# Three ternary weight buffers and a hand-given VectorE order in the gated stage of a hybrid block

## The chip, the cores and the metric

One core of a Trainium2 chip runs the kernel. The metric is the device time of one execution in microseconds, lower is better. Engines are named as in the profile: PE (TensorE matmuls), PEld (its weight loads), DVE (VectorE), ACT (ScalarE), POOL (GpSimd) and SP (SyncE, which here issues the DMAs). 128x512 means 128 partitions by 512 elements.

## The reference

A block of four residual steps on x of 2 x 1024 rows by D = 512; each step takes the layernorm of x.

```python
x = x + attn_a(layernorm(x), w_in, w_out)     # gated stage
x = x + ffn(layernorm(x), w_gate_up, w_proj)  # feed-forward 0
x = x + attn_b(layernorm(x), ...)             # softmax attention
x = x + ffn(layernorm(x), w_gate_up, w_proj)  # feed-forward 1

# attn_a: 16 heads of 32, chunks of 64 rows
q, k, v, a, g = split(x @ w_in.T, 5)
q = q * rsqrt(mean(q*q) + eps);  k = tanh(k)
a = clip(sigmoid(a + 2), 0.6, 0.9995);  u = k * v
prefix = cumprod(a)                            # inside a chunk
mem = prefix * (state + cumsum(u / max(prefix, 1e-6)))
y = sigmoid(g) * (q * mem) + (1 - sigmoid(g)) * v
return y @ w_out.T

# ffn: the weights are made ternary in groups of 64
scale = mean(abs(w));  w = clip(round(w / scale), -1, 1) * scale
h = silu(x @ w_gate.T) * (x @ w_up.T)
return rms_norm(h) @ w_proj.T
```

## The kernel before, in words

The change lies in the first stage (the gated attention, L182 to L430) and in its border with feed-forward 0.

The 2048 rows are four units t of 512 rows. x stays in SBUF as 16 tiles of 128 rows (xres). For a unit, `Input` measures the rows (layernorm statistics on DVE, a square root on ACT), scales them (`normal`, xn_a on DVE), and PE transposes them (`turn`, xnt_a) for ACT to copy (a_xt). `queries` (L273) then projects q in four column tiles c, squares it on ACT, and sums the squares per head on PE (pss); a root on ACT and three DVE steps (L300 to L304) make the factor rq. The loop over t and c (L335 to L407) projects k and v (kv), a and g (ag), each 8 matmul calls for a half of 512 columns; PE's order is the program's. Behind the projections stands a chain for each c: ACT makes u, v, a and gate; DVE clips a, scans it (prefix), POOL multiplies u by prefix, DVE scans again (mem), multiplies by qn (L391, from pr, a product on PE that spreads rq over the heads) and by gate, and POOL subtracts and adds v, which gives yt. In the very last chain the POOL steps are on DVE (`other`, L366). After the four c come the output products a_out (L421), in which yt is multiplied by w_out, and DVE adds them to x (L426). The queries of the next unit are put ahead of these output products.

In the gaps of this stage the feed-forward weights are made ternary. `Ternary` (L144) holds one chunk f of 16: three tiles of 128x512 loaded to the tile w (L155), their absolute values mag (L157) and signs (L159) on ACT; `mean` (L162) is a small product pm on PE and a copy to scale on ACT; `finish` (L169) is six DVE steps over 128x1536 (L171 to L179). `quantise(0..2)` does the means, `quantise(3)` finishes the chunk, stores it to DRAM (L319) and begins the next, whose load waits for a buffer. w, mag, sign and scale have two buffers each. At L345 `pieces` says which of these calls stands behind which projection.

Feed-forward 0 begins with 16 loads of those chunks into SBUF (L569) and with the layernorm and transposition of its first four tiles (xn_f, xnt_f, xs, L570 to L573); the statistics of these tiles are taken in the last unit (L398). Each chunk is then 8 matmuls g, 8 u and 8 f_out.

What sets the order: PE follows the program in the gated stage (`manual_schedule`, L323) until `order.close()` (L415). DVE follows it only for the first input (L326); elsewhere the scheduler places DVE, ACT, POOL and SP instructions by its own estimates when the kernel is built, and each engine then works its queue in the order built. PSUM for single products and transpositions is a pool of four banks (`bank`), for kv and ag two tiles (`big`).

Of the kernel before, what the change touches and what calls it, by code (L numbers as in the profile page):

```python
# [17 lines left out]
P = 128  # L18
D = 512
# [23 lines left out]
def kernel(  # L43
# [31 lines left out]
    def bank(name):  # L75
        return ps_pools[-1][1].tile([P, BLK], F32, tag="bank", name=name)
# [4 lines left out]
    def load_x(lo, hi):  # L81
        for i in range(lo, hi):
            nc.sync.dma_start(out=xres[i], in_=x[ts(i, P), :])
# [55 lines left out]


# [3 lines left out]
    class Ternary:  # L144
# [3 lines left out]
        def __init__(self, pool, f, tiles):  # L148
            self.pool, self.f, self.n = pool, f, f"{f}_{tiles[0]}"
            self.shape = [P, len(tiles), D]  # L150
            self.w = pool.tile(self.shape, F32R, tag="w32", name=f"w32_{self.n}")
            w32 = self.w.bitcast(F32)
            for i, e in enumerate(tiles):
                src = w_pt[ts(f, P), :] if e == 2 else w_gu[e * NF + f].rearrange("p c n -> p (c n)")
                nc.sync.dma_start(out=w32[:, i, :], in_=src)  # L155
            self.mag = pool.tile(self.shape, BF, tag="mag", name=f"mag{self.n}")
            nc.scalar.activation(self.mag, w32, AF.Abs)  # L157
            self.sign = pool.tile(self.shape, BF, tag="sign", name=f"sign{self.n}")
            nc.scalar.sign(self.sign, w32)  # L159
            self.scale = None  # L160

# [20 lines left out]
    with ExitStack() as s:  # L182
# [8 lines left out]
        def load_w_in(i):  # L191
            w = w_in.tile([P, NKC, D], F32, tag=f"w_in{i}", name=f"w_in{i}")
            nc.sync.dma_start(
                out=w, in_=w_in_t[:, ts(i, D)].rearrange("(c p) n -> p c n", p=P)
            )
            return w

        w_q, w_k, w_v = (load_w_in(i) for i in range(3))
# [6 lines left out]
        chunk = [Ternary(tp, 0, range(3))]  # L205
        w_a, w_g = (load_w_in(i) for i in (3, 4))
        load_x(TPB, 2 * TPB)
        w_out = wa.tile([P, NKC, D], F32, name="w_out")
        nc.sync.dma_start(out=w_out, in_=w_out_t.rearrange("(c p) n -> p c n", p=P))

# [62 lines left out]
        def queries(t, xt):  # L273

            q = ap_.tile([P, NKC, BLK], F32, tag="q", name=f"q{t}")
            pss = bank(f"pss{t}")
            late = []

            def mean_square(c, sq):
                nc.tensor.matmul(  # L280
                    pss, headmean[:, c, :], sq, start=(c == 0), stop=(c == NKC - 1)
                )

            for c in range(NKC):
                pq = bank(f"pq{t}_{c}")
                project(pq, w_q, c, xt)
                nc.scalar.copy(q[:, c, :], pq)
                sq = ap_.tile([P, BLK], F32, tag="sq", name=f"sq{t}_{c}")
                nc.scalar.square(sq, pq)
                if late:  # L290
                    mean_square(*late.pop())
                late.append((c, sq))
                if c < 3 and t:
                    quantise(c)
                elif c and not t:
                    quantise(c - 1)
            mean_square(*late.pop())
            rq = ap_.tile([16, BLK], F32, tag="rq", name=f"rq{t}")
            nc.scalar.activation(rq, pss[:16, :], AF.Sqrt, bias=rms_eps[:16])
            nc.vector.reciprocal(rq, rq)  # L300
            parts = rq_parts[t % 2]
            hi, lo = parts[:16], parts[32:48]
            nc.vector.tensor_copy(hi, rq)
            nc.vector.tensor_sub(lo, rq, hi.bitcast(F32))  # L304
            quantise(3)
            return q, parts

        load_x(2 * TPB, NTT)

        def quantise(i):  # L310

            now = chunk[0]
            if now is None:
                return
            if i < 3:
                now.mean(i, bank)
                return
            now.finish(now.w)
            nc.sync.dma_start(out=w_kept[now.f].bitcast(F32), in_=now.w.bitcast(F32))  # L319
            chunk[0] = Ternary(tp, now.f + 1, range(3)) if now.f + 1 < NF else None  # L320

        order = ExitStack()
        order.enter_context(tc.manual_schedule(engines={mybir.EngineType.PE}))  # L323
        before = [None] * NKC
        first = Input(0, at_once=False)
        with tc.manual_schedule(engines={mybir.EngineType.DVE}):  # L326
            for j in range(TPB + 1):
                if j < TPB:
                    first.measure(j)
                if j:  # L330
                    first.normal(j - 1)
                    first.turn(j - 1)
        xt = first.xt
        q, rq = queries(0, xt)
        for t in range(NBLK):  # L335
            yt = wa.tile([P, NKC, BLK], F32, tag="yt", name=f"yt{t}")
            following = None
            for c in range(NKC):
                n = f"{t}_{c}"
                kv, ag = big(f"kv{n}"), big(f"ag{n}")  # L340
                project(kv[:, 0, :], w_k, c, xt)
                project(kv[:, 1, :], w_v, c, xt)

                if t < NBLK - 1:
                    pieces = ((2,), (), (3,)) if c % 2 else ((0,), (1,), ())  # L345
                else:
                    pieces = ((0, 1), (2,), (3,)) if c < NKC - 1 else ((), (), ())
                for i in pieces[0]:
                    quantise(i)
                project(ag[:, 0, :], w_a, c, xt)  # L350
                project(ag[:, 1, :], w_g, c, xt)
                for i in pieces[1]:
                    quantise(i)
                if following and c > 1:
                    for j in (2 * c - 4, 2 * c - 3):
                        following.turn(j)
# [9 lines left out]
                other = nc.gpsimd if (t, c) < (NBLK - 1, NKC - 1) else nc.vector  # L366
# [12 lines left out]


# [6 lines left out]

                pr = bank(f"pr{n}")
                nc.tensor.matmul(pr, headrow[:, c, :], rq, start=True, stop=True)
                qn = ap_.tile([P, BLK], F32, tag="qn", name=f"qn{n}")  # L390
                nc.vector.tensor_mul(qn, pr, q[:, c, :])  # L391
# [4 lines left out]

                if t + 1 == NBLK and c == 0:
                    ff_stats = layernorm_stats(range(TPB), "f0_0")  # L398
                if t + 1 < NBLK and c < 2:
                    if c == 0:  # L400
                        following = Input(t + 1)
                    following.normal(0 if c == 0 else 1)
                for i in pieces[2]:
                    quantise(i)
                if following and c == 2:
                    following.normal(2)
                    following.normal(3)  # L407

            if following:
                xt = following.xt  # L410
                q_next, rq_next = queries(t + 1, xt)
            products = [(j, k) for j in range(TPB) for k in range(NKC)]
            if not following:

                order.close()  # L415
                products.sort(key=lambda jk: jk[1] == NKC - 1)
            po = {}
            for j, k in products:
                if k == 0:
                    po[j] = bank(f"a_out{t}_{j}")  # L420
                nc.tensor.matmul(  # L421
                    po[j], yt[:, k, ts(j, P)], w_out[:, k, :], start=(k == 0), stop=(k == NKC - 1)
                )
                if k == NKC - 1:
                    xi = xres[t * TPB + j]
                    nc.vector.tensor_add(xi, xi, po[j])  # L426
                    if following:
                        quantise(j)
            if following:
                q, rq = q_next, rq_next  # L430

    edge_sb = ctx.enter_context(tc.tile_pool(name="edge", bufs=1, reuse_waits="tile"))
# [20 lines left out]
    class FeedForwardInput:  # L455


        def __init__(self, which, t, pool, tag, stats=None):
            self.n = f"{which}_{t}"
            self.which, self.tiles = which, range(t * TPB, (t + 1) * TPB)  # L460
            self.stats = stats or layernorm_stats(self.tiles, f"f{self.n}")
            self.xs = pool.tile([P, 2, NKC, BLK], F32R, tag=tag, name=f"xs{self.n}", bufs=1)
            self.xn = {}

        def normal(self, j):
            i = self.tiles[j]
            self.xn[j] = normal(i, j, self.stats, f"f{self.which}_{i}")

        def tile(self, j, psum):
            if j not in self.xn:  # L470
                self.normal(j)
            pt = transposed(self.xn.pop(j), f"f{self.which}_{self.tiles[j]}", psum)
            hi, lo = (self.xs[:, e, :, ts(j, P)] for e in range(2))
            nc.scalar.copy(hi, pt)  # L474
            nc.vector.tensor_sub(lo, pt, hi.bitcast(F32))

# [5 lines left out]
    def feed_forward(which, store, first=None, beside=None):  # L482


        with ExitStack() as s:
# [84 lines left out]
            if not first:  # L570
                first = FeedForwardInput(which, 0, edge_sb, "xt", ff_stats)
                for j in range(TPB):
                    first.tile(j, ring)  # L573
# [44 lines left out]
        0, False, None,  # L618
# [533 lines left out]
```

## Time and profile before

| what | value |
|---|---|
| median of 3 runs | 2147.88 us (2146.33 to 2148.32) |
| profiled execution | 2146.65 us |
| its span, first to last instruction | 2144.9 us |
| mean granted PE clock | 0.996 |
| PE's idle time from 0 to 420 us | 23.5 us |
| gated stage: first q product to last output product | 12.38 to 393.44 us |
| first product of feed-forward 0 | 398.59 us |

The page says for every engine how long it was busy in the span; a view of waits says which engine waited for which instruction of which other one; a timeline lists instructions with their start and duration, and in brackets the idle time before them with what ended it. "x16" counts instructions: a matmul call on 32-bit data is two instructions. In a windows row the columns are: stretch, its length, PE, PEld, DVE, ACT and POOL busy (with counts), granted PE clock, share of DMA, GB/s. Idle time of an engine costs nothing unless PE or the end waits for it.

### The profile page before, as it was taken

Reading aid. Unit: us, or ns where it says so; the run is one execution under the profiler, and the core shown is the slowest. Engines: PE = TensorE matmul, PEld = TensorE weight load, DVE = VectorE, ACT = ScalarE, POOL = GpSimd, SP = SyncE. Lnnn points to the kernel's source line nnn. Section 1 sums busy time; section 2 is a strip of 40 time slices with the busy share of each in tenths; the row PEclk is TensorE's granted clock in tenths of the full one; section 3 lists DMA queues with packets and bytes.
Section 4 is the critical chain, followed back from the end, with each engine's and each line's share of the span. In section 5 each row is a group of like instructions: output and inputs, shape, how many; then the busy total and the mean of one; then the engine's idle time right before and its main releaser. Section 6 shows DMA issues by size and latency. Waiting matters only on the chain.

```text
span 2144.9 us, 28054 instructions
## 1 busy us (share of the span) xinstructions
PE 2108.8 (98%) x10615; PEld 1242.2 (58%) x10624; DVE 1069.1 (50%) x2272; ACT 835.2 (39%) x1590; POOL 449.8 (21%) x812
## 2 busy tenths in 40 slices
PE   8999999999999999999999999999999999999998
PEld 3444444688888854444444444444545447888887
DVE  5766686533343234555555465464546662433322
ACT  4444333234344322444444422243434523333333
POOL 1312212122122221111111113021212221121212
PEclk9999999999999999999999999999999999999999
DMA  6111211600000111111110101201110033000000
GB/s 255 59 59 62 86 59 74 250 1 1 1 1 1 35 46 37 41 26 41 23 44 21 46 8 37 57 20 42 24 32 15 14 111 132 20 1 20 1 20 20
DMA packets 50999, 98.71 MB, mean 46 GB/s; under 512 B 10800, under 2 KB 19120, under 8 KB 50864
## 3 DMA queue, kind: packets, MB, share of 16 engines
q1 hardware_dynamic: 50864, 96.93, 13.8%
q8 instruction: 83, 1.36, 0.3%
q14 instruction: 52, 0.43, 0.1%
HBM read 58.75 MB, written 16.78 MB: 35 GB/s over the span
## 4 chain that ended last, share of the span: by engine, by line
PE 83%; DVE 8%; DMA 4%; ACT 2%; issue 1%; POOL 1%; SPq 1%; DVEq 0%; ACTq 0%; POOLq 0%
PE y L904 12%; PE g L524 11%; PE u L524 11%; PE f_out L545 11%; PE s L805 10%; PE pq L737 8%; PE t L866 8%; PE pv L702 3%; PE b_out L965 2%; DMA w<-in_w_pt_dram 1%; DMA w_kept<-w 1%; DVE one L174 1%; PE kv L269 1%; DVE w L179 1%; PE ag L269 1%
## 5 line engine op out<-in xcount | busy, mean ns | idle before, releaser
L882 ACT ACTIVATE pr<-t 128x512 f32<-128x512 f32 (+3 forms) x768 | 314.8, 497 | 380.6 <-PE t L874 380.4
L815 DVE CUSTOM_DVE_ANT_0 s<-s,causal 128x128 f32<-128x128 f32 (+3 forms) x512 | 245.3, 510 | 126.1 <-PE s L805 117.4
L904 PE MATMUL y<-pr,val 128*64 128x512 f32 (+3 forms) x1536 | 291.6, 501 | 0.2 <-POOL pr L885 0.2
L539 POOL TENSOR_TENSOR ssq<-ssq,sq 128x512 f32<-128x512 f32 x120 | 155.9, 1299 | 603.6 <-ACT sq L538 603.6
L530 DVE TENSOR_TENSOR h<-h,u 128x512 f32<-128x512 f32 x128 | 88.0, 688 | 362.0 <-PE u L524 355.9
L524 PE MATMUL g<-xs,w 128*128 128x512 f32 x1024 | 262.4, 398 | 0.9 <-ACT xs L474 0.7
L545 PE MATMUL f_out<-w,hs 128*128 128x512 f32 x1024 | 257.7, 394 | 0.3 <-DVE hs L533 0.3
L820 DVE TENSOR_REDUCE nmax<-s 128x1 f32<-128x512 f32 x256 | 165.0, 686 | 184.4 <-PE s L805 184.3
L524 PE MATMUL u<-xs,w 128*128 128x512 f32 x1024 | 256.4, 392 | 0.0
L805 PE MATMUL s<-gr,gr 32*128 32x512 f32 (+3 forms) x1536 | 248.8, 492 | 2.6 <-DVE nmax L815 2.6
L524 PEld LDWEIGHTS u<-xs,w 128*128 128x128 f32 x1024 | 192.4, 188 | 43.5
L545 PEld LDWEIGHTS f_out<-w,hs 128*128 128x128 f32 x1024 | 191.6, 188 | 43.9 <-DVE hs L533 1.1
L524 PEld LDWEIGHTS g<-xs,w 128*128 128x128 f32 x1024 | 190.9, 189 | 44.0 <-ACT xs L474 0.9
L866 PE MATMUL t<-gr,gr 32*128 32x512 f32 (+3 forms) x1536 | 198.8, 533 | 0.0
L904 PEld LDWEIGHTS y<-pr,val 128*64 128x64 f32 x1536 | 93.5, 136 | 179.9 <-issue 105.7
L737 PE MATMUL pq<-b_xt,w_qk 128*128 128x512 f32 x384 | 176.0, 603 | 0.0
L805 PEld LDWEIGHTS s<-gr,gr 32*128 32x128 f32 x1536 | 147.6, 185 | 46.8 <-issue 14.0
L532 ACT CAST hs<-h 128x512 fp32r<-128x512 f32 x128 | 79.4, 621 | 236.6 <-DVE h L530 236.6
L885 POOL TENSOR_SCALAR_AFFINE_SELECT pr<-pr 128x256 f32<-128x256 f32 x256 | 101.3, 408 | 332.2 <-ACT pr L882 332.2
L529 ACT ACTIVATE h<-g 128x512 f32<-128x512 f32 x128 | 76.5, 598 | 224.3 <-PE g L524 224.1
L533 DVE TENSOR_TENSOR hs<-h,hs 128x512 fp32r<-128x512 f32 x128 | 88.6, 692 | 83.1 <-ACT hs L532 83.1
L737 PEld LDWEIGHTS pq<-b_xt,w_qk 128*128 128x128 f32 x384 | 69.6, 189 | 88.0 <-issue 74.0
(155 smaller groups left out, 2211.0 us busy)
## 6 DMA issues: line engine op xcount, KB each, us to landing
w<-w_kept SPq DMA_DIRECT2D x32, 768.0 KB, 8.7
w_kept<-w SPq DMA_DIRECT2D x16, 768.0 KB, 3.2
gr<-gr SPq DMA_DIRECT2D x96, 128.0 KB, 2.3
w<-in_w_gu_dram SPq DMA_DIRECT2D x32, 256.0 KB, 2.8
share<-ys SPq DMA_DIRECT2D x128, 64.0 KB, 2.0
w_in<-in_w_in_t_dram SPq DMA_DIRECT2D x5, 1024.0 KB, 11.2
x<-in_x_dram SPq DMA_DIRECT2D x16, 256.0 KB, 7.1
w<-in_w_pt_dram SPq DMA_DIRECT2D x16, 256.0 KB, 3.5
```

The source lines that it names most:

```text
L524: nc.tensor.matmul(po, ws[f][:, part, ts(k, P)], xs[:, e, k, :], start=(k == 0 and e == 0), stop=(k == NKC - 1 and e == 1),)
L533: nc.vector.tensor_sub(hp[:, 1, :], h, hp[:, 0, :].bitcast(F32))
L539: nc.gpsimd.tensor_add(ssq, ssq, sq)
L545: nc.tensor.matmul(po[j], hp[:, e, ts(j, P)], ws[f][:, 2, :], start=(f == 0 and e == 0), stop=(f == NF - 1 and e == 1),)
L737: nc.tensor.matmul(po, w[:, k, ts(kind, P)], xts[b][:, k, ts(e, BLK)], start=(k == 0), stop=(k == NKC - 1),)
L805: nc.tensor.matmul(part, queries[:, ts(j, P)], keys[:, first : first + nk], start=True, stop=True,)
L815: nc.vector.tensor_tensor_reduce(part, part, causal[:, BLK - part.shape[-1] :], -1.0, 3.0e38, ALU.add, ALU.min, top,)
L820: nc.vector.tensor_reduce(top, part, AX.X, ALU.max, negate=True)
L866: nc.tensor.matmul(banks[u, e][:, :nq], keys[:, ts(kb, P)], queries[:, (qb + 1) * BLK - nq : (qb + 1) * BLK], start=True, stop=False,)
L882: nc.scalar.activation(pr[:, e, :nq], banks[u, e][:, :nq], AF.Exp)
L885: nc.gpsimd.affine_select(out=pr[:, :, :P], in_=pr[:, :, :P], compare_op=ALU.is_ge, fill=0.0, base=0, pattern=[[0, 2], [1, P]], channel_mu ...
L904: nc.tensor.matmul(y[64 * e : 64 * e + 64, lo:], all_values[:, HV * (NH * kb + h) : HV * (NH * kb + h) + 64], pr[:, e, : BLK - lo], start= ...
```

## The change

Five edits, all in the gated stage and at its end.

1. The ternary weight tile w gets three buffers. Loading (`__init__`) and the work on it (`begin`) are parted; chunks 1 and 2 are loaded at the start, and finishing chunk f issues the load of f+3. w_q and w_k move to the pool `edge`, into the space that the feed-forward's first input takes later.
2. DVE's order is the program's in the whole stage (`fixed`). qn is written over q and is placed before the second scan; the next unit's input is measured at the end of the unit before.
3. The last sum of squares, the root (`roots`) and the factor (`factors`) go behind the first and second output product; transpositions of the next input stand between kv and ag.
4. Feed-forward 0's first input is made in the last unit: it is measured behind c=1 (two tiles normalised there), its tiles are transposed in c=3, two before ag and two between its halves.
5. Chunk 15 is finished behind the last additions to x; the last output products take k in the order (0, 1), 2, 3.

```diff
-            self.w = pool.tile(self.shape, F32R, tag="w32", name=f"w32_{self.n}")
+            self.w = pool.tile(self.shape, F32R, tag="w32", name=f"w32_{self.n}", bufs=3)
...
+        def begin(self):
...
+        w_qk = edge_sb.tile([P, 2, NKC, D], F32, tag="xt", name="w_in_qk")
...
-        chunk = [Ternary(tp, 0, range(3))]
+        chunk = [Ternary(tp, 0, range(3)).begin()]
         w_a, w_g = (load_w_in(i) for i in (3, 4))
         load_x(TPB, 2 * TPB)
+        chunk.append(Ternary(tp, 1, range(3)))
...
+        chunk.append(Ternary(tp, 2, range(3)))
...
+            rq = ap_.tile([16, BLK], F32, tag="rq", name=f"rq{t}", bufs=1)
+            def roots():
+                mean_square(*late.pop())
+                nc.scalar.activation(rq, pss[:16, :], AF.Sqrt, bias=rms_eps[:16])
+            def factors():
+                nc.vector.reciprocal(rq, rq)
...
-            chunk[0] = Ternary(tp, now.f + 1, range(3)) if now.f + 1 < NF else None
+            chunk.pop(0)
+            if chunk:
+                chunk[0].begin()
+            if now.f + 3 < NF:
+                chunk.append(Ternary(tp, now.f + 3, range(3)))
...
-        order.enter_context(tc.manual_schedule(engines={mybir.EngineType.PE}))
+        fixed = {mybir.EngineType.PE, mybir.EngineType.DVE}
+        order.enter_context(tc.manual_schedule(engines=fixed))
...
-                    pieces = ((0, 1), (2,), (3,)) if c < NKC - 1 else ((), (), ())
+                    pieces = (((0, 1), (2,), (3,)), ((0, 1), (2,), ()), ((), (), ()))[max(c - 1, 0)]
...
+                if not last and c > 1:
+                    for j in (2 * c - 4, 2 * c - 3):
+                        following.turn(j)
+                        if c == 2:
+                            following.normal(j + 2)
                 for i in pieces[0]:
                     quantise(i)
+                ff_tiles = range(TPB) if last and c == NKC - 1 else ()
+                turn = lambda name: bank(name)
+                for j in ff_tiles[:2]:
+                    ff_first.tile(j, turn, j + 2)
                 project(ag[:, 0, :], w_a, c, xt)
+                for j in ff_tiles[2:]:
+                    ff_first.tile(j, turn)
                 project(ag[:, 1, :], w_g, c, xt)
...
+                if last and c == NKC - 3:
+                    ff_first = FeedForwardInput(0, 0, edge_sb, "xt")
+                    ff_first.normal(0)
+                    ff_first.normal(1)
...
-                order.close()
-                products.sort(key=lambda jk: jk[1] == NKC - 1)
+                products.sort(key=lambda jk: max(jk[1], 1))
...
+                    if not last:
+                        if j == 0:
+                            roots()
+                        elif j == 1:
+                            factors()
                         quantise(j)
+            if last:
+                quantise(3)
+            if not last:
                 q, rq = q_next, rq_next
+                following = Input(t + 2) if t + 2 < NBLK else None
+        order.close()
```

The class `FeedForwardInput` moves ahead of the stage and takes a tile to normalise between the two steps of another:

```diff
+        def tile(self, j, psum, following=None):
...
             nc.scalar.copy(hi, pt)
+            if following:
+                self.normal(following)
             nc.vector.tensor_sub(lo, pt, hi.bitcast(F32))
```

## The prediction

> **What bounds the kernel now.** First the page: which engine is full. Then PE's waits in the stage that the change touches (0 to 420 us), since only they can be won.
>
> ```profile
> PE 2108.8 (98%) x10615; PEld 1242.2 (58%) x10624; DVE 1069.1 (50%) x2272; ACT 835.2 (39%) x1590; POOL 449.8 (21%) x812
> ```
>
> PE is busy 98% of the span: 36 us are idle in all, 23.5 of them before 420 us, and 6.8 of these before the first transposition. The other stages are not touched. PE's waits, in total us, times, longest:
>
> ```profile
> PE pm L166 <- ACT mag L157: 4.7, 2, 2.7
> PE pss L280 <- ACT sq L289: 3.4, 5, 2.1
> PE pq L269 <- ACT a_xt L265: 2.6, 4, 0.7
> PE xnt_f L136 <- DVE xn_f L127: 2.3, 2, 1.9
> PE a_out L421 <- POOL yt L395: 1.0, 1, 1.0
> ```
>
> pm on mag is the late ternary load (40 us and 352 us). The next view is the timeline at the second of these and at the end of the stage, with PE's clock in two windows of 2 us (the third number from the end):
>
> ```profile
> 355.06 1.01 PE L166 MATMUL pm<-mag,groupmean 128*128 128x512 bf16 x2 [2.68 <-ACT mag L157]
> ...
> 355.87 8.17 PE L269 MATMUL ag<-a_xt,w_in 128*128 128x512 f32 x16
> ```
>
> ```profile
> 356.00:358.00 2.00, 2.00 (x4) 0.88 (x3) 1.01 (x1) 2.00 (x5) 0.95 (x1) 0.50 0.04 8
> ```
>
> ```profile
> 376.73 0.33 SPq L319 DMA_DIRECT2D w_kept<-w  x1
> 377.17 19.11 SPq L569 DMA_DIRECT2D w<-w_kept  x16
> ...
> 393.49 0.69 DVE L426 TENSOR_TENSOR x<-x,a_out 128x512 f32<-128x512 f32 x1 [0.17 <-PE a_out L421]
> ...
> 397.29 0.63 PE L136 MATMUL xnt_f<-ident,xn_f 128*128 128x128 f32 x4 [1.95 <-DVE xn_f L127]
> ...
> 402.48 2.06 PE L524 MATMUL u<-xs,w 128*128 128x512 f32 x8
> ```
>
> After 2.68 us of idleness PE runs 3.4 us at half clock: the 16 ag matmuls take 8.17 us, 7.03 elsewhere. And feed-forward's 16 weight loads leave SP at 377.17, behind the last ternary store and 16 us ahead of the end of the output products (393.44), so they are hidden. Last, DVE's price for finishing a chunk, with POOL beside it and without:
>
> ```profile
> 58.85 2.70 DVE L174 SCALAR_TENSOR_TENSOR one<-scale,mag 128x1536 bf16<-128x1536 bf16 x1
> ...
> 59.90 2.78 POOL L367 TENSOR_TENSOR u<-u,v 128x512 f32<-128x512 f32 x1
> ...
> 125.71 1.76 DVE L174 SCALAR_TENSOR_TENSOR one<-scale,mag 128x1536 bf16<-128x1536 bf16 x1
> ```
>
> **What is removed.** Three weight buffers, issued one or two chunks ahead, remove the waits on mag (2.06 and 2.68) and the half clock behind the second (8.17-7.03, and 0.4 in the two pm: 1.55). pss of the last square goes behind the first output product, transpositions go ahead of ag: gone are five pss waits (3.4, one of them 2.07 because mag sat ahead of sq on ACT), three pq on a_xt (1.9), one pq on scale (0.68). yt for k=2 is no longer needed first (1.01). Sum 13.3 us. w_qk in another pool, rq with one buffer and qn written over q move no work; their waits are on long finished readers, cost 0 (cover: a whole unit; without it one 0.7 us multiplication). On SP six ternary loads move ahead of w_out and eight x tiles (1.6 MB, 3.9 us at the 408 GB/s of that time): first needed at 113 and 80 us, cost 0. On DVE the statistics of unit 1 stand ahead of the first rq and wait for x (landed from 23.2 on), rq's root is there at about 36: cost 0.
>
> **Output products of units 0 to 2.** In the new order DVE finishes two chunks (chains' last, then the queries') before it adds the first a_out to x, and the second pm after it needs that bank. From the end of ag (c=3): chain 0.7+7.9 (row 67.19 to 75.66 without qn), finish 8.0 (POOL only beside its first step) = 16.6. ACT holds the next sign until then (two sign buffers), copies q and scale: 18.7. Second finish 7.1, add 0.7: 26.5. PE is there at 0.4+18.2-0.9+3.4+0.9+0.2+3.4 = 25.5. A new wait of about 1.2, three times: 3.7 (0 to 6; below nothing is excluded, since PE has nothing to gain there but the waits counted above).
>
> **Last unit: DVE in the given order.** Zero is the end of ag for c=0 (330.3 in the trace). Before, chain and finish interleave, so POOL's answers are hidden: 334.47 to 376.6 holds three of each, 14.0 a pair. Given in order, a chain takes 7.9 (the two POOL answers are waited for), and a finish behind it meets POOL's yt and u*v: 58.26 to 67.27 is 9.0, 88.43 to 98.76 without foreign steps 8.5; I take 8.7. So: 0.7+7.9+8.7 = 17.3. ACT's sign for the chunk two ahead waits for the end of that finish and stands before c=1's sigmoid: 1.5+0.7+0.1 more, 19.6. Chain and finish: 36.2. Now comes what the change moves here, the measuring of feed-forward's first input; the built order shows four further statistics of block 1 and one of block 2 drawn in with it: 8x0.66+7x0.13 = 6.2, then 0.17+0.66+0.54: the first xn_f is there at 43.8. ACT's square root (table load 1.28) lies beside the statistics. PE wants it at 14.6+14.6+7.5 = 36.7 (two units of kv and ag as between 330.30 and 344.91, then kv): **wait 7.1**. Queued behind it on PE is all of c=3 and the output. Then xn_f 0.5, c=2's chain 7.9 with 0.8 of drawn-in statistics, xn_f of tile 2: 53.6; PE without a stop would be at 43.8+1.0+3.4 = 48.2, at half clock up to 50.6: it goes on at 53.6, 12.4 later than unstalled; tile 3 costs 0.7, the half clock after the second gap 1.5. **Sum 14.6.** From below: if pairs took 14.0 as now, 0.7+28.0+6.2+1.4 = 36.3, no wait at all. From above: the SBUF page.
>
> There the Trainium skill speaks against the change (SBUF — State Buffer, Who interferes with whom): DVE with two SBUF inputs and GpSimd share a port pair, and the loser blocks fully. By the rule a finish is 7.0+1.27+1.27 = 9.5 and the wait 1.6 longer; the rows give +0.9 for one POOL step (2.70 to 1.76), 8.7. I take the rows.
>
> For the half clock the row is stricter than the skill (TensorE: Matmul & The Clock Gate, What's actually happening), which lets an idle window of about 3.4 us throttle: here 2.68 us did, 2.07 (205.79) did not. By the rule the second gap (2.8 to 5.2) might cost nothing, by the row 1.5; taken: 1.5.
>
> **Transpositions** of feed-forward's tiles move ahead of the output: 2x1.04 = 2.1 more of PE before its end, and 2.1 less behind (in the next sum).
>
> **The last chunk.** DVE now finishes chunk 15 behind the four adds to x, and SP, which takes its issues in order (it waits 155.3 us in ten places for DVE's w in this stage, the next loads behind it), has the 16 weight loads behind that chunk's store. Zero is the end of the output products. Adds: the last ends at 0.9. Finish without POOL 0.6+1.8+3x0.98+1.76, and one drawn-in statistic 0.7: 8.7. SP 0.03+0.41 (376.70 to 377.17): 9.1. The first load lands 5.6 after its issue (377.17, the same store ahead of it): 14.7. Then half clock, 1.55 by the row at 355 to 2.45 by the first 16 matmuls of the kernel (9.32 instead of 6.87): 2.4. So PE loses 17.2 (below 15, if the load takes the 4.0 that the fastest did; above 18.5). Before, 393.44 to u at 402.66 is 9.2, of it 1.87 eight g matmuls: 7.35. **Cost 9.85.** PE, and through it everything, waits here; the later loads (0.77 MB at about 420 GB/s, 1.9 us) keep ahead of PE's 5.6 us a chunk.
>
> **Sum**: -13.3+3.7+14.6+2.1+9.85 = +17.0. On the profiled execution's 2146.65: 2163.7; the median of the runs lies 1.2 higher: 2164.9.
>
> **Rivals.** (a) DVE keeps pace in the last unit: the interleaving was worth nothing, pairs take 14.0, only the end of the stage costs. -13.3+3.7+2.1+9.85 = +2.4: 2150.3. For it: DVE has 66.6 of 90 us busy from 310 to 400. Against it: POOL's answers are idle time that DVE can't fill in a given order.
> (b) Faster: the store of chunk 15 doesn't hold the loads, so w_0 lies in SBUF when the products end. Place: SP's queue. The end then costs about 0.5 instead of 7.35; with DVE as in (a) -13.3+3.7+2.1-6.85 = -14.35: 2133.5. It decides once the first load lands less than 0.5 us after the products; and the wait in the last unit has to stay under 10 us for the sign to turn to clearly faster. Against it: the order of SP's issues, and 155.3 us of such waits.
> (c) Worse: the ring DVE finish, ACT mag and sign, DVE scale stops PE some 4 us in each of the units 0 to 2 and half clock follows (1.55): 3x4.3 more, 2178.
> That the change doesn't do what it says is excluded for the loads: chunk 1 is issued before w_out.
>
> **Chances.** Forecast 0.70 (2154 to 2172 with finish 7.5 to 9.5, load 4.0 to 6.5, output waits 0 to 6), (a) 0.14, (b) 0.07, (c) 0.09. Within 0.2% is within 4.3 us, about what a measurement of this kernel can tell from no change. Faster is (b): 0.07; same most of (a): 0.09; slower the rest: 0.84. The range 2151 to 2173 leaves out (b), half of (c) and some of (a).
>
> **What will show it.** A PE wait on xn_f of about 7 us in the last unit, a second of 3 to 5 one projection later; SP's first weight load some 9 us behind the last output product and PE idle 14 to 15 us there, clock 0.50 in both places; no PE wait on mag; pm in the output products on DVE's add of x about 1 us. I am wrong if SP issues the weights before the products end, or if xn_f is there before kv of c=3 ends.

## The result, and the profile after

| what | before | after |
|---|---|---|
| median of 4 runs each | 2147.57 us (2146.33 to 2148.32) | 2170.53 us (2168.92 to 2174.70) |
| profiled execution | 2146.65 us | 2169.54 us |
| mean granted PE clock | 0.996 | 0.991 |
| first kv product of unit 3 starts at | 316.13 us | 320.57 us |
| last output product ends at | 393.44 us | 407.56 us |

The changed kernel is slower: ratio 1.011, 95% interval 1.0093 to 1.0128. The profiled executions differ by 22.9 us, all of it before the second block of feed-forward 0. A word on the counts: a half of kv or ag, and a tile of a_out, are four matmul calls and eight instructions (x8 in the lines), not eight calls; g, u and f_out are eight calls and eight instructions. First the page's line of busy time, then PE's waits from 0 to 440 us (total us, times, longest), which answer to the list of before:

```profile
PE 2112.7 (97%) x10615; PEld 1244.6 (57%) x10624; DVE 1077.9 (50%) x2272; ACT 833.1 (38%) x1588; POOL 450.5 (21%) x812
```

```profile
PE g L564 <- DMA w<-w_kept: 14.4, 1, 14.4
PE xnt_f L136 <- DVE xn_f L127: 10.2, 3, 7.3
...
PE a_out L477 <- ACT rq L343: 5.3, 3, 3.0
PE pm L196 <- DVE x L482: 2.9, 3, 1.0
PE pss L320 <- ACT sq L329: 1.0, 3, 0.6
```

The waits on mag, on scale and on yt are gone, pss's are down from 3.4 to 1.0. The line of g is new, that of xn_f has grown from 2.3 us, and that of pm (2.9) is new: these three were forecast. The line `a_out <- ACT rq` is new and was not. The timeline places them. At the end of the stage (PE and SP; the brackets hold the idle time before):

```profile
378.73 1.97 PE L136 MATMUL xnt_f<-ident,xn_f 128*128 128x128 f32 x8 [7.30 <-DVE xn_f L127]
380.49 5.43 PE L308 MATMUL ag<-a_xt,w_in 128*128 128x512 f32 x8
388.10 0.66 PE L136 MATMUL xnt_f<-ident,xn_f 128*128 128x128 f32 x4 [2.18 <-DVE xn_f L127]
...
416.24 7.78 SPq L609 DMA_DIRECT2D w<-w_kept  x10
...
421.93 3.56 PE L564 MATMUL g<-xs,w 128*128 128x512 f32 x8 [14.37 <-DMA w<-w_kept]
```

PE waits 7.30 us for the first xn_f; the ag after it takes 5.43 instead of 3.60, half clock for part of it (granted 0.66); the tile after that is late by another 2.18. The output products end at 407.56, DVE finishes chunk 15 at 415.8, SP sends the first weight load at 416.24, and the first g starts at 421.93 (before: 398.59). Between units 2 and 3, where almost nothing was forecast (SP, ACT, PE):

```profile
297.79 0.33 SPq L360 DMA_DIRECT2D w_kept<-w  x1
302.93 0.80 SPq L181 DMA_DIRECT2D w<-in_w_gu_dram  x2
...
307.39 1.48 ACT L186 ACTIVATE mag<-w 128x1536 bf16<-128x1536 f32 x1 [6.65 <-DMA w<-in_w_pt_dram]
...
310.19 0.68 ACT L343 ACTIVATE rq<-pss,rms_eps 16x512 f32<-16x512 f32 x1
...
310.92 6.16 PE L477 MATMUL a_out<-w_out,yt 128*128 128x512 f32 x8 [2.98 <-ACT rq L343]
```

Read it from the top. A chunk is finished and its store is sent at 297.79; the load of the chunk three further on goes into the same buffer, waits until the store has landed, and leaves SP only at 302.93, 5.1 us later (SP waits 38.8 us in thirteen places for a store's end before such a load). In units 0 and 1 the same step took 3.2 us (107.45 to 110.68, 201.94 to 205.18); why this store took longer the profile doesn't show, and one store of the kernel before took 5.1 too (192.50). ACT has the mag of that load ahead of the root, waits 6.65 us for it, and the root ends at 310.9. PE's third output product needs the PSUM bank that the root reads, and waits. Half clock follows: 6.16 us for what takes 3.60 elsewhere, at a granted clock of 0.59. In the windows view of the whole stretch the granted clock (third number from the end) is 0.81:

```profile
303.00:320.57 17.57, 13.61 (x28) 5.60 (x26) 10.12 (x10) 6.34 (x7) 0.00 (x0) 0.81 0.40 134
```

### The profile page after: what moved, and what is told of

Same layout as the page of the kernel before. It is cut to its first block, busy times and chain, and to the rows that moved or that the text cites. A ratio compares the mean times of both kernels' runs of the same rounds, so it can differ in the third digit from the quotient of the medians.

```text
span 2167.8 us, 28032 instructions
## 1 busy us (share of the span) xinstructions
PE 2112.7 (97%) x10615; PEld 1244.6 (57%) x10624; DVE 1077.9 (50%) x2272; ACT 833.1 (38%) x1588; POOL 450.5 (21%) x812
## 4 chain that ended last, share of the span: by engine, by line
PE 90%; DVE 5%; DMA 2%; ACT 1%; POOL 1%; issue 1%; SPq 0%; DVEq 0%; ACTq 0%; POOLq 0%
PE y L940 12%; PE g L564 11%; PE u L564 11%; PE f_out L585 11%; PE s L841 10%; PE pq L773 8%; PE t L902 8%; PE ag L308 4%; PE kv L308 4%; PE pv L738 3%; PE b_out L1001 2%; PE a_out L477 2%; PE mt L881 1%; PE t L910 1%; PE pq L308 1%; DVE one L204 1%
## 5 line engine op out<-in xcount | busy, mean ns | idle before, releaser
L564 PE MATMUL g<-xs,w 128*128 128x512 f32 x1024 | 262.1, 398 | 14.4 <-DMA w<-w_kept 14.4
```

The costliest lines, as they stand in the source:

```text
L564: nc.tensor.matmul(po, ws[f][:, part, ts(k, P)], xs[:, e, k, :], start=(k == 0 and e == 0), stop=(k == NKC - 1 and e == 1),)
```

## The experiments

Theory after this reading: the loss has three seats. (1) The border: chunk 15's store stands ahead of the weight loads on SP. (2) The last unit: DVE's given order, block behind block, brings xn_f late. (3) The output products of units 0 to 2: ACT's work for the next chunks stands ahead of what PE needs from ACT. Rivals are the prediction's (a), that DVE keeps pace in the last unit, (b), that the store doesn't hold the loads, and (c), the ring; and against (3), that PE waits there for DVE itself. The kernel before ran beside each group of experiments (medians 2149.19, 2147.74 and 2146.93). The changed kernel did not, so differences to its median of 2170.53 are sure to about 2 us only. And the scheduler places ACT's instructions anew in every build: an edit of DVE's order can act through ACT's.

| run | edit against the changed kernel | median us | ratio to before, 95% interval |
|---|---|---|---|
| e1 | store of chunk 15 on POOL's queue | 2158.78 | 1.0051 (1.0036 to 1.0066) |
| e2 | first tiles measured at the end of unit 2 | 2166.19 | 1.0083 (1.0065 to 1.0101) |
| e3 | root ahead of the output products | 2170.85 | 1.0107 (1.0091 to 1.0122) |
| e4 | chunk 15 finished behind c=2 | 2162.60 | 1.0070 (1.0057 to 1.0084) |
| e5 | DVE's order left to the scheduler | 2138.78 | 0.9958 (0.9943 to 0.9972) |
| e6 | e3 and three buffers for mag and sign | 2158.04 | 1.0046 (1.0033 to 1.0059) |
| e7 | (kernel before) three weight buffers alone | 2154.26 | 1.0034 (1.0022 to 1.0046) |
| e8 | given order alternating, e1, e2 | 2138.18 | 0.9954 (0.9942 to 0.9967) |
| e9 | e5 and e6 | 2151.24 | 1.0017 (1.0008 to 1.0025) |
| e10 | e8 and e6 | 2137.34 | 0.9951 (0.9938 to 0.9963) |
| e11 | given order alternating alone | 2157.10 | 1.0045 (1.0033 to 1.0058) |

### The border: e1 and e4

```diff
-            nc.sync.dma_start(out=w_kept[now.f].bitcast(F32), in_=now.w.bitcast(F32))
+            (nc.sync if now.f < NF - 1 else nc.gpsimd).dma_start(out=w_kept[now.f].bitcast(F32), in_=now.w.bitcast(F32))
```

> The changed kernel (2169.5 us profiled, 2170.5 median), with the store of chunk 15 alone issued from POOL's queue instead of SP's. My theory (the store stands ahead of feed-forward's weight loads on SP): the 16 loads leave SP before the output products end, PE goes from the last output product to g in about 0.5 us instead of 14.4 with half clock behind it, gain 15 to 15.5: about 2155. DVE still finishes the chunk 8.7 us after the products, which then delays the first h a little (0 to 2). Rival (the first load is held by SBUF that the gated stage still uses, not by the queue): w_0 still lands some 14 us after the products, within 2 us of 2170. Nothing moves in the last unit or in the output products of units 0 to 2.

Measured: 2158.78, 11.7 less than the changed kernel. SP and PE in the timeline of e1:

```profile
371.87 50.78 SPq L609 DMA_DIRECT2D w<-w_kept  x16
...
406.62 2.43 PE L564 MATMUL g<-xs,w 128*128 128x512 f32 x8
...
416.71 0.50 PE L585 MATMUL f_out<-w,hs 128*128 128x512 f32 x1 [2.06 <-ACT hs L572]
```

The loads leave SP at 371.87, 44 us sooner, and g follows the output products at once; it is POOL now that holds the store until DVE is done (415.73), and no load stands behind it. So the store on SP is the cause, and rival (b) falls in this kernel: the store does hold the loads. The gain is 11.7 and not 15 because the finish itself stays: DVE makes the first h behind it, and f_out waits 2.3 us, with some half clock.

```diff
-                    pieces = (((0, 1), (2,), (3,)), ((0, 1), (2,), ()), ((), (), ()))[max(c - 1, 0)]
+                    pieces = ((0, 1), (2,), (3,)) if c < NKC - 1 else ((), (), ())
...
-                quantise(3)
+                pass
```

> The changed kernel with chunk 15 finished where the kernel before had it, behind c=2 of the last unit (here, in the given order, end to end behind that chain and ahead of the third tile of xn_f). My theory (in the given order DVE has no room there; at the end of the stage the finish holds SP, here it holds xn_f): the second wait on xn_f grows from 2.2 to about 11 us, while the weight loads leave SP some 15 us ahead of the products' end and the border loses its 16 us: 2170.5 + 8.9 - 16 = about 2163. Rival (moving the chunk to the end was pure loss): xn_f's waits stay at 10.2 in all, 2154.5.

Measured: 2162.60, as the theory has it: the loads leave SP at 396.61, 21 us ahead of the first g (417.48), which waits for nothing. PE and SP in the timeline of e4:

```profile
396.61 26.17 SPq L609 DMA_DIRECT2D w<-w_kept  x16
...
396.67 2.17 PE L136 MATMUL xnt_f<-ident,xn_f 128*128 128x128 f32 x8 [9.89 <-DVE xn_f L127]
```

The finish of 8.9 us costs PE nearly its whole length wherever it stands in a given, block-wise order: ahead of the third xn_f (a wait of 9.89 in place of 2.18, 7.7 more), or ahead of the weight loads (14.37, of which 8.7 pass until SP may send them).

### The last unit: e2 and e5

```diff
-                following = Input(t + 2) if t + 2 < NBLK else None
+                following = Input(t + 2) if t + 2 < NBLK else layernorm_stats(range(TPB), "f0_0")
```

(and the two normals of c=1 ahead of `quantise`).

> The changed kernel with the statistics of feed-forward's first tiles given to DVE at the end of unit 2 (where DVE is idle from 328.5 us to the first chain) and the first two normals ahead of chunk 14's finish. My theory (DVE's whole given order of the last unit is late, statistics 6.4 us of it, and the third tile stands behind chunk 14's finish of 8.9 and a chain of 7.9): the first wait of 7.3 us on xn_f is gone, the second grows from 2.2 to 5 to 6, as PE comes there sooner, and half clock follows (1.7). Gain 4.5 to 6.5: about 2165. Rival 1 (the statistics alone made PE wait): all waits on xn_f go, gain 13: 2157.5. Rival 2 (the time is only paid elsewhere): within 1 us of 2170.5.

Measured: 2166.19; PE in the timeline of e2:

```profile
382.41 1.12 PE L136 MATMUL xnt_f<-ident,xn_f 128*128 128x128 f32 x4 [6.47 <-DVE xn_f L127]
...
384.73 5.37 PE L308 MATMUL ag<-a_xt,w_in 128*128 128x512 f32 x8
```

The first wait is gone (xnt_f at 371.47) and the next is 6.47 long, for PE now comes earlier to a tile that is bound by all of DVE's work before it. The statistics are 6.4 us of the delay, not the delay.

```diff
-        fixed = {mybir.EngineType.PE, mybir.EngineType.DVE}
+        fixed = {mybir.EngineType.PE}
```

> The changed kernel with DVE's order left to the scheduler (as in the kernel before), all else as changed. In the order built the statistics and first two normals stand ahead of the last unit's finishes, finish and chain alternate step by step in the last unit, and chunk 15's last step stands ahead of the last chain. My theory (the given order is what costs, in the last unit and, through the late store, at the border): no wait on xn_f over 1 us (-13) and the loads leave SP before the products end (-15); the waits on ACT's root and half clock (10.5) stay: about 2142.5. Rival (DVE has too much work in the last unit in any order): waits on xn_f of 5 us or more stay, 2150 or more. If pm's waits on DVE's add (2.9) go too, DVE's order made them.

Measured: 2138.78, faster than both kernels. DVE in the last unit, and SP, in the timeline of e5:

```profile
329.29 0.42 DVE L428 TENSOR_SCALAR a<-a 128x512 f32<-128x512 f32 x1
329.62 0.55 DVE L201 TENSOR_SCALAR scale<-scale 128x1536 bf16<-128x1536 bf16 x1
...
344.53 1.18 DVE L428 TENSOR_SCALAR a<-a 128x512 f32<-128x512 f32 x1
...
377.83 23.00 SPq L609 DMA_DIRECT2D w<-w_kept  x16
```

Steps of the chain (L428) and of the finish (L201) alternate, and the next clip of a comes at 344.53, 15.2 us later. In the changed kernel the first such pair takes 19.1 (sign ahead of the sigmoid on ACT included) and the second 16.9 (up to the statistics at 371.70):

```profile
335.66 0.43 DVE L428 TENSOR_SCALAR a<-a 128x512 f32<-128x512 f32 x1 [7.16 <-ACT a L422]
...
354.78 0.43 DVE L428 TENSOR_SCALAR a<-a 128x512 f32<-128x512 f32 x1 [2.12 <-ACT a L422]
```

The loads leave at 377.83, 16 us ahead of the products' end. What is left: 4.4 us on xn_f, 5.0 of pss on sq with half clock. The output products of units 0 to 2 lost their waits as well, which I had not expected of DVE's order. ACT's built order differs there too: between units 2 and 3 the mag ahead of the root (305.11) waits 0.47 us for DVE, and none that waits for its load stands there.

### The output products: e3 and e6

```diff
                 q_next, rq_next, roots, factors = queries(t + 1, xt)
-                quantise(3)
+                roots(), quantise(3)
...
-                            roots()
+                            pass
```

> The changed kernel with the last mean square and the root of the next unit's queries ahead of the output products of units 0 to 2, instead of behind the first of them. My theory (ACT's root stands behind the mag of the chunk two ahead, which waits for DVE and for its load, and pss's bank is what the third output product waits for): the waits of a_out on ACT's root (5.3 us) and the half clock behind them (5.2) go, new pss waits on sq of 0.5 to 1 us come three times, pm's waits on DVE's add (2.9) stay. Gain 7 to 9: about 2162.5. Rival (PE waits there for DVE, which finishes two chunks in a row, and the root is only named last): the waits move to pm or to the next bank, gain under 2: 2169 or more.

Measured: 2170.85, no gain; my theory's number failed. (The first kv of unit 3 starts 1.5 us sooner, but PE then waits 11.3 us for xn_f instead of 10.2, and 14.7 for g.) ACT and PE between units 0 and 1 in e3:

```profile
104.56 1.48 ACT L186 ACTIVATE mag<-w 128x1536 bf16<-128x1536 f32 x1 [4.99 <-DVE scale L207]
...
109.68 0.61 ACT L329 ACTIVATE sq<-pq 128x512 f32<-128x512 f32 x1
...
110.35 1.54 PE L320 MATMUL pss<-sq,headmean 128*128 128x512 f32 x2 [2.15 <-ACT sq L329]
```

The waits on the root and on DVE's add are gone, and PE waits 2.15 us for a square instead, with half clock behind (the next a_out takes 4.92). That square stands on ACT behind a mag (104.56) and a sign (107.35) which wait for DVE to finish the chunk whose buffers they take. So ACT is held twice: by mag and sign through their own two buffers, and then by the next mag through its load. The rival has the number, but PE waits for ACT. Whether DVE's adds would be late as well can't be read here, as PE comes later. e6 removes both holds:

```diff
-            self.mag = pool.tile(self.shape, BF, tag="mag", name=f"mag{self.n}")
+            self.mag = pool.tile(self.shape, BF, tag="mag", name=f"mag{self.n}", bufs=3)
...
-            self.sign = pool.tile(self.shape, BF, tag="sign", name=f"sign{self.n}")
+            self.sign = pool.tile(self.shape, BF, tag="sign", name=f"sign{self.n}", bufs=3)
...
-            one = self.pool.tile(self.shape, BF, tag="one", name=f"one{self.n}", bufs=1)
+            one = self.w.bitcast(BF)[:, :, :D]
...
-                mem = ap_.tile([P, BLK], F32, tag="mem", name=f"mem{n}")
+                mem = ap_.tile([P, BLK], F32, tag="mem", name=f"mem{n}", bufs=1)
```

> The changed kernel with three buffers instead of two for mag and sign (the room comes from keeping DVE's helper tile in the weight tile's own space and from one buffer for mem), so that ACT no longer waits for DVE's finish, and with the root ahead of the output products as in the run before. My theory (in units 0 to 2 PE waits, through ACT's squares, copies and root, for a mag or sign that stands ahead on ACT and waits for DVE's finish): the waits on ACT's root and on DVE's add (5.3 and 2.9) and the half clock behind them (5.2) go, and the pss waits of 2.15 that the root alone put in their place go too; waits on xn_f shrink by up to 2.6, since sign no longer holds c=1's sigmoid in the last unit. Border as in the changed kernel. 2170.5 - 13.4 - 1 to 3: about 2155. Rival (DVE itself is what PE waits for there, two finishes of 16 us in a row): pm or a_out wait for DVE's add to x for 2 to 4 us in each unit, gain under 5: 2166 or more.

Measured: 2158.04. PE's waits of e6 from 0 to 440 us:

```profile
PE xnt_f L136 <- DVE xn_f L127: 9.0, 3, 5.1
...
PE pm L196 <- ACT scale L197: 1.6, 1, 1.6
PE pss L320 <- ACT sq L329: 1.0, 3, 0.3
```

Of the 9.2 us of waits at the output products (5.3, 2.9 and 1.0) 2.6 are left (1.6 and 1.0), without half clock, and DVE, which finishes the same two chunks in a row, is waited for no more: its second finish no longer waits 2.0 us for ACT's scale. The first kv of unit 3 starts at 309.77 and no longer at 320.57, so 10.8 of the 12.5 us are won here. The border is untouched (g waits 14.4). So at (3) PE waits for ACT, held by mag and sign, and not for DVE's own work. The root alone (e3) does not do it; whether the buffers alone would, no run shows.

### Parts alone and together: e7, e8, e11, e9, e10

e7 is the kernel before with the first edit alone, and what makes room for it (qn over q, one buffer for rq).

> The kernel before with the first edit alone: three weight buffers, loads one or two chunks ahead, w_q and w_k in the other pool, and what makes the room (qn over q, one buffer for rq); DVE's order stays with the scheduler, all else as before. My theory (of the 13.3 us of removed gaps the buffers account for the waits on mag and the half clock behind the second, 6.3): 2147.9 - 6.3 = 2141.6. Rival 1 (mag then waits for its own buffer, that is for DVE's finish, and PE with it): within 2 us of the kernel before. Rival 2 (the buffers are harmful in themselves, e.g. as begin is pulled ahead on ACT): slower than before.

Measured: 2154.26, slower than before: my number failed; it is rival 1's mechanism with rival 2's sign. ACT and PE at the end of unit 0 in e7:

```profile
94.97 1.48 ACT L160 ACTIVATE mag<-w 128x1536 bf16<-128x1536 f32 x1 [5.96 <-DVE scale L181]
96.36 1.05 ACT L277 COPY a_xt<-xnt_a 128x512 f32<-128x512 f32 x2
...
97.46 6.55 PE L281 MATMUL pq<-a_xt,w_in_qk 128*128 128x512 f32 x8 [4.82 <-ACT a_xt L277]
```

In the kernel before the copy comes first and mag long behind it:

```profile
93.66 1.06 ACT L265 COPY a_xt<-xnt_a 128x512 f32<-128x512 f32 x2
...
106.43 1.48 ACT L157 ACTIVATE mag<-w 128x1536 bf16<-128x1536 f32 x1 [2.61 <-DVE mem L394]
```

In e7 the scheduler places mag sooner on ACT, presumably because by its estimate the weights are there. There mag waits for its own buffer, DVE's finish again, and what stands behind it is the copy that PE's next queries need (4.82, 3.12 and 3.28 us at the three borders of units). So the buffers alone do not pay; which of the other edits they need no run parts.

e11 and e8 keep the order given, but spread the six finishing steps over the chain:

```diff
+                steps = chunk[0].finish(chunk[0].w) if 3 in pieces[2] else iter(())
-                nc.vector.tensor_scalar(a, a, A_MIN, A_MAX, ALU.max, ALU.min)
+                nc.vector.tensor_scalar(a, a, A_MIN, A_MAX, ALU.max, ALU.min), next(steps, 0)
...
-                nc.vector.tensor_copy(start[:, 0:BLK:CHUNK], a[:, 0:BLK:CHUNK])
+                nc.vector.tensor_copy(start[:, 0:BLK:CHUNK], a[:, 0:BLK:CHUNK]), next(steps, 0)
```

(and so on behind both prefix steps, the second scan and the state copy; `finish` yields its steps).

> The changed kernel with DVE's order still given, but in a better one: the six finishing steps of a chunk stand one by one between the steps of the chain of the same column tile, the statistics of feed-forward's first tiles stand at the end of unit 2, and chunk 15's store goes out on POOL's queue. My theory (it is the order end to end that costs, not that an order is given: a pair of chain and finish takes 19.6 us end to end, 15 to 16 alternating): no wait on xn_f, border as in the run with the store aside; 2170.5 - 13 - 11 = 2146.5, less 0 to 3 in the output products of units 0 to 2, whose ring stays. Rival (pairs are as long as before, ACT's sigmoid sets them): xn_f still waits 4 us or more, 2152 or more.

> The changed kernel with the alternating order of chain and finish alone (statistics and store stay where the change put them). It parts the gain of 32 us of the run with all three. My theory: the two pairs of the last unit end about 8 us sooner, so the first wait on xn_f (7.3) goes, a second of 3 to 4 stays, as 6.4 us of statistics and a chain still stand ahead of it, with half clock behind (1.5); in units 0 to 2 the finish ends sooner, ACT's mag and sign with it, and the waits on ACT's root shrink as in that run to 2.7, without half clock: -10 there, -6.5 in the last unit, border as it was: about 2154. Rival (the ring needs the other two edits, or the statistics alone were worth those 6.4): 2160 or more.

Measured: 2138.18 for e8, 8 below what I had expected, and 2157.10 for e11, between its two cases. PE's waits on a_out and xn_f in e8, then those on g and xn_f in e11, whose a_out waits the same 2.7:

```profile
PE a_out L478 <- ACT rq L344: 2.7, 3, 1.0
...
PE xnt_f L136 <- DVE xn_f L127: 1.8, 2, 1.1
```

```profile
PE g L565 <- DMA w<-w_kept: 15.1, 1, 15.1
...
PE xnt_f L136 <- DVE xn_f L127: 6.9, 3, 4.8
```

A given order is not what costs; a given order end to end is. Alternating alone gains 13.4, in the output products (2.7 instead of 9.2, no half clock) and in the last unit, less 1.7 us of new waits on xn_a. The statistics and the store give the other 19. The first wait on xn_f of e11, 1.8 us where I said none, is the size I missed.

e9 joins e5 and e6:

> The changed kernel with DVE's order left to the scheduler, three buffers for mag and sign, and the root ahead of the output products: the candidate that should beat both kernels. My theory: against 2138.8 with the scheduler's order alone, the two pss waits on sq (5.0) and the half clock behind them (about 3) go, the waits on xn_f (4.4) stay: about 2131. Rival (the ring of two buffers costs nothing once DVE alternates; what is left is the start of the queries): 2138 or more.

Measured: 2151.24, a miss by 20. ACT in the last unit of e9:

```profile
337.11 1.48 ACT L186 ACTIVATE mag<-w 128x1536 bf16<-128x1536 f32 x1 [5.14 <-DVE q L443]
...
340.38 0.69 ACT L422 ACTIVATE a<-ag,two 128x512 f32<-128x512 f32 x1
```

In this build mag stands on ACT ahead of the sigmoid that starts the chain, presumably because a third buffer lets it; a starts 4.5 us after ag's end (335.84), where in e5 it starts at once (328.23 behind 328.19), the chain is as much later, and PE waits 5.50 us for xn_f's third tile, 3.6 more than in e5. The queries of units 1 to 3 lost 7.3 us besides, waiting for DVE (the view names the copy to a_start, right behind the step that reads pr's bank). With DVE's order given and alternating, the same edits do no harm:

> The best version so far (given order, alternating; statistics early; store on POOL; 2138.2) with three buffers for mag and sign and the root ahead of the output products besides. My theory: the last waits on ACT's root (2.7) go, nothing else moves: 2135.5, which is at the edge of what can be told. Rival (as in the run with a free DVE order, which these two edits made 12 us slower: more room lets ACT's mag and sign run ahead of the sigmoids that the chains wait for): 2141 or more.

Measured: 2137.34. The waits on the root are gone, and 1.0 us on a square came for them; the interval and that of e8 overlap, so that the two can't be told apart. e5, e8 and e10 beat both kernels, by 0.4 to 0.5% against the kernel before.

## Why the prediction was right

The sum forecast 2164.9, the runs gave 2170.5. By its own steps, in the profiled executions:

| stretch | predicted | measured |
|---|---|---|
| start to the first kv of unit 3 | -8.04 + 3.7 = -4.3 | 320.57 - 316.13 = +4.4 |
| from there to the last output product | -2.68 - 1.55 - 1.01 + 14.6 + 2.1 = +11.5 | 14.1 - 4.4 = +9.7 |
| border | +9.85 | 22.9 - 14.1 = +8.8 |

**The removed gaps**, 13.3: right for the changed kernel, each of them is gone (the 1.0 us of pss waits that it still has is counted in the next item). But e7 shows that the three buffers, to which I put the half of it, do not earn it alone: the wait on the load turns into one on mag's buffer.

**The output products**, 3.7: this is the term that was mis-sized. Measured: 9.2 us of waits (0.97 of pm each time, where I said 1.2; a_out on the root 1.14, 1.21 and 2.98; pss 1.0) and half clock in two of the three places (5.40 and 6.16 in place of 3.60), 4.4: 13.6 in all, 9.9 more than forecast. The step that failed says that the second pm waits for DVE's add, and looks no further: I followed DVE, and left the root on ACT at nothing, without pricing what stands ahead of it there. It is the third buffer's own load, which is sent only when a chunk is finished and stored, and so the late load that I had counted as removed came back ahead of the root. In unit 2 that store took 1.9 us longer than in the others, which is about what a_out waits longer there. Rival (c) had the place and about the size (4 us and half clock in each unit; measured 2.3, 2.8 and 4.1 before half clock), but another path: through sq or the root on ACT, not through DVE's scale.

**The last unit**, 14.6: right. The wait was 7.30 (7.1), and ACT's sign stood ahead of c=1's sigmoid as forecast. Waits and half clock together were 13.0 (7.30, 2.18 and 0.75; 1.97-1.04 and 5.43-3.60). The second wait was 2.18 and not 3 to 5, because half clock had made PE later there. The 1.5 of half clock behind the second gap did not come: ag took 3.60 there, as the clock rule that the prediction weighs against its row allowed. Rival (a) falls: in e5 DVE keeps nearly pace (15.2 a pair against PE's 14.6), but only as chain and finish alternate. Its 14.0 a pair was too short, too: from 334.47 to 376.6 the third chain is not at its end. From clip to clip the pairs of the kernel before took 14.7, 15.9 and 15.2.

The finish with POOL beside it took 8.9, nearer to the 8.7 of the rows than to the 9.5 that the prediction works out from the port rule it cites. But the rows do not speak against the rule, only against that sum. These two lines of the kernel before stand around those that the prediction shows:

```profile
58.42 1.51 POOL L395 TENSOR_TENSOR yt<-mem,v 128x512 f32<-128x512 f32 x1 [0.80 <-DVE mem L394]
...
61.58 1.91 DVE L176 TENSOR_TENSOR scale<-scale,mag 128x1536 bf16<-128x1536 bf16 x1
```

POOL's step ends at 59.93, and the DVE step begun at 58.85 ends 1.62 behind it, about its own 1.76. POOL's next ends at 62.68, 1.13 behind that DVE step (alone 1.27), and DVE's next at 63.49, 0.81 behind that (alone 0.96). So each looks held until the other's step is nearly over (POOL's times are rough), and DVE lost only the rest of a POOL step under way, 0.94 and 0.95, where the sum took two whole ones of 1.27.

**The border**, 9.85: right, measured 8.8: DVE done 8.2 after the products and SP's load issued 8.7 after (9.1), first g 14.4 after (14.7), then half clock, 1.5 where 2.4 was forecast.

The parts add up to -13.3 + 13.6 + 13.0 + 2.1 + 8.8 = 24.2 for measured 22.9; 0.6 of the difference is the very first 16 products (8.70 instead of 9.32 us, half clock in both), the rest is not placed. That the sum came within 5.6 us of the median is in part luck: of the 9.9 missed at the output products the last unit, the border and the first products, each cheaper than forecast or before, took back 3.3.

## What to carry to other kernels

When a load comes earlier, ask what its consumer now stands in front of on its own engine: an operation that waits at the head of an in-order queue delays everything behind it, and PE waited here for a copy, a square and a root in place of the load's first consumer. A given order of an engine is as good as its interleaving: two chains that each wait for another engine belong step by step between each other. A store that waits for the last result should not stand ahead of loads on the same queue.

## What the runs showed of the hardware that was not expected

Half clock does not follow from the length of a gap. In the changed kernel, after 0.97 and 1.21 us with a product of 0.38 between, eight products took 5.40 us instead of 3.60 (granted clock 0.68); after 0.97 and 1.14, 3.70 (1.00):

```profile
118.73 3.70 PE L477 MATMUL a_out<-w_out,yt 128*128 128x512 f32 x8 [1.14 <-ACT rq L343]
...
213.29 5.40 PE L477 MATMUL a_out<-w_out,yt 128*128 128x512 f32 x8 [1.21 <-ACT rq L343]
```

In e7 a gap of 3.12 us was followed by 5.39, one of 3.28 by 3.70:

```profile
195.37 5.39 PE L281 MATMUL pq<-a_xt,w_in_qk 128*128 128x512 f32 x8 [3.12 <-ACT a_xt L277]
...
292.28 3.70 PE L281 MATMUL pq<-a_xt,w_in_qk 128*128 128x512 f32 x8 [3.28 <-ACT a_xt L277]
```

What decides between them no run here tells, so that a forecast can give only a range for it.
